# Weights of a 3x3 convolution behind two tiles' softmax, two small inputs by other queues, and a twelfth work tile

## The chip, the cores and the metric

The kernel runs on one core of one Trainium2 chip. The core has five engines that run side by side, each with its own queue that is worked through in order: TensorE (PE in the profile; its weight loads are PEld), VectorE (DVE), ScalarE (ACT), GpSimd (POOL) and SyncE (SP), which here only issues DMA transfers. GpSimd issues DMA transfers too. The engines wait for each other by semaphores. The metric is the time on the device in microseconds, the median of several runs; less is better. The profile shows one execution.

## The reference

The input x has the shape (2, 256, 64, 64). Two layers follow each other, each as x = x + layer(group norm of x), with 32 groups of 8 channels.

Layer 0 is self-attention with 8 heads of 32 channels over all 4096 positions of an image:

```python
qkv = einsum('bchw,oc->bohw', x, qkv_w) + qkv_b
w = softmax(einsum('bhci,bhcj->bhij', q, k) / sqrt(32), axis=-1)
out = einsum('bhij,bhcj->bhci', w, v)
```

Layer 1 has two branches on the same normalised input. The first is attention within sets of 64 positions, done twice: over positions 8 apart (queries and keys from 1x1 convolutions with a position term, then a 1x1 convolution, scale, shift and relu give `feats`), and then within 8 by 8 blocks, with two 1x1 convolutions and relu each for queries and keys, one for values, one for the output. The second branch mixes the heads of q, k and v by a 9 by 12 matrix and applies a grouped 3x3 convolution. The output is rate1 times the first branch plus rate2 times the second.

```python
f_all = einsum('bidn,oi->bodn', concatenate([qh, kh, vh], 1), fc_w)
out_conv = conv_general_dilated(f_conv, dep_w, (1, 1), ((1, 1), (1, 1)), feature_group_count=hd)
return rate1 * out_att + rate2 * out_conv
```

## The kernel before, in words

All of it is in `direct_layers`. Images are done one after the other (the batch index b is 0, then 1), each as eight tiles of 512 positions by 256 channels, two halves of 128 channels (KC = 2) on the partitions.

**Order of the work.** Pools give out buffers: `work` has 11 tiles of 4 KB per partition that everything short-lived shares (`w4`), `xpool` nine tiles of x, `const` what stays. A tile waits until the last reader of the buffer's previous tenant is done. The order of instructions on an engine is made by a scheduler from the program's order and its own estimates, except inside `manual_schedule`, which keeps the written order on the engines it names; `issue_after` sets an instruction behind another one. SP's and GpSimd's DMA issues stand in their queues like other instructions.

**Start.** SP loads the rows of w1 and w2 (L86), `place_rows` (L90) and the eight tiles of x (`load_x`, L70). GpSimd clears and loads small things: at_query, masks, `grid` (L169), at last `meet` (L209). `fold_scores` folds two 1x1 convolutions of layer 1 into one matrix: two transposes (L192), a small product, `meet` filled by ScalarE, a product of `meet` and `grid` (pt_key, L215), and the products pt_g (L204), copied to wt_g and kept in memory. VectorE meanwhile takes statistics of x (`group_stats`, L308, L312); their means over groups are a matmul (pm_l, L315), which follows the fold in TensorE's queue. Then VectorE normalises x (L350), and `project0` projects queries, keys and values (L400, L423).

**Attention of layer 0** (`attention0`): sixteen groups of scores, exponentials on ScalarE (L499), products with the values (L509), sums on VectorE (L546) and by adding DMA transfers of GpSimd (L556).

**Layer 1, first attention** (`layer1_first`). `group_attention` is a generator in parts: scores (sp, L1006), values (pvs, L988), softmax on VectorE and ScalarE (L1022 to L1029: nm, e, den); then transposes of the weights (at, L1034) and their copy into `bd` (L1043); then the products pc (L1052). In batch 0, `conv_weights` is called after it. It makes the 3x3's weights: three small loads, products with the mixing matrix, and for each half of the channels 9 taps of 12 scaled additions (L845, L847), then sums and differences of the taps (L851 to L858). The result goes to memory by 32 stores of SP (L860). `kept["made"]` is the last of these operations.

**Layer 1, second attention and convolution** (`layer1_second`). For each tile t, `branch` makes queries (phq, prq: L1262, L1271), another call makes keys (phk, prk), then come scores, softmax, at and pc as above. Between these stand the 16 steps of the convolution, four positions of four strips, where `spots` says: place 0 after the queries, 1 after the scores, 2 after pc. A step (`conv`) makes the next strip's input on GpSimd (`conv_transform`: L911 col, L915 v), then 32 matmuls (mm, L925), a copy by ScalarE and sums on VectorE (z, L930 to L934; into x, L946 to L952). All mm use one accumulator, so one waits for the z of the last. The first step loads all weights back (L875), transposes them on TensorE (pw, L884) and scales them (L887, L889). `to_image` (ScalarE, L1221) writes the padded image xp, whose first row VectorE clears in batch 0 (L1213). `conv_edges` (L959) corrects the borders of x by small additions. When a strip's four steps are done, its two output tiles are finished (L1321) and stored (L1324), which also frees x for batch 1: SP loads the next x (L70), and VectorE takes its statistics (L308).

Of the kernel before, what the change touches and what calls it, by code (L numbers as in the profile page):

```python
# [17 lines left out]
P = 128  # L18
# [4 lines left out]
KC = C // P  # L23
# [17 lines left out]
def direct_layers(ctx: ExitStack, tc: tile.TileContext, a: dict, out: bass.AP, bad: bass.AP):  # L41
# [7 lines left out]
    apool = ctx.enter_context(tc.tile_pool(name="apool", bufs=1))  # L49
    kpool = ctx.enter_context(tc.tile_pool(name="kpool", bufs=2))  # L50
    vpool = ctx.enter_context(tc.tile_pool(name="vpool", bufs=1))
    work = ctx.enter_context(tc.tile_pool(name="work", bufs=11))
    small = ctx.enter_context(tc.tile_pool(name="small", bufs=2))
    wpool = ctx.enter_context(tc.tile_pool(name="wpool", bufs=3))
    cpool = ctx.enter_context(tc.tile_pool(name="cpool", bufs=1))
# [24 lines left out]
    for name in ("w1", "w2"):  # L80
        by_out[name] = wpool.tile([P, KC, C], F32, tag="wp", name=f"{name}_by_out")

        for i in range(4):
            for half in range(2):
# [1 line left out]
                nc.sync.dma_start(  # L86
                    out=by_out[name][r : r + 32, i // 2, :], in_=a["wx"][int(name == "w2"), half, i, 0:P:4, :]
                )
    place_rows = const.tile([4, C], F32, name="place_rows")
    nc.sync.dma_start(out=place_rows, in_=a["posq"])  # L90
    x_first = load_x(0)

    ident = const.tile([P, P], F32, name="ident")
# [71 lines left out]
    nc.gpsimd.memset(at_query, 0.0)  # L165
    masks = const.tile([P, 2], F32, name="masks")
    nc.gpsimd.memset(masks, 0.0)
    grid = const.tile([2, 64], F32, name="grid")
    nc.gpsimd.dma_start(out=grid, in_=a["loc"][1:3, 0:64])  # L169
    for u in range(4):  # L170
        r = HD0 * u
        for half in range(2):
# [11 lines left out]
    def fold_scores():  # L184


        wts["g"] = wpool.tile([P, KC, C], F32, tag="wp", name="wt_g_0")

        place = const.tile([P, KC, 4], F32, name="place")
        pp = bank([P, KC, 4], "pt_place")  # L190
        for k in range(KC):
            nc.tensor.transpose(pp[:, k, :], place_rows[:, k * P : (k + 1) * P], ident[0:4, 0:4])  # L192
        nc.scalar.copy(place, pp)

        part = const.tile([P, KC, 3], F32, name="query_part")
        for k in range(KC):
            nc.scalar.activation(
                part[:, k, 0:1], place[:, k, 0:1], AF.Identity, bias=place[:, k, 3:4], scale=0.125
            )
        nc.scalar.copy(part[:, :, 1:3], place[:, :, 1:3])  # L200

        def product(dst, lhs, rhs):
            for j in range(KC):
                nc.tensor.matmul(dst, lhs(j), rhs(j), start=j == 0, stop=j == KC - 1)  # L204

        pm = bank([2, 3], "pt_meet")
        product(pm, lambda j: place[:, j, 1:3], lambda j: part[:, j, :])
        meet = const.tile([2, P], F32, name="meet")
        nc.gpsimd.memset(meet, 0.0)  # L209
        by_four = meet.rearrange("j (u r) -> j u r", u=4)  # L210
        nc.scalar.copy(by_four[:, :, 0:2], ident[0:2, 0:2].unsqueeze(1).to_broadcast([2, 4, 2]))
        for u in range(4):
            nc.scalar.copy(by_four[:, u, 2:AT], pm)
        pk = bank([P, 64], "pt_key")
        nc.tensor.matmul(pk, meet, grid, start=True, stop=True)  # L215
        nc.scalar.copy(at_key, pk)
        for k in range(KC):
            block = slice(k * P, (k + 1) * P)
            pg = bank([P, C + AT], f"pt_g_{k}")
            product(pg[:, 0:C], lambda j: by_out["w1"][:, j, block], lambda j: by_out["w2"][:, j, :])  # L220
            product(pg[:, C : C + 2], lambda j: by_out["w1"][:, j, block], lambda j: place[:, j, 1:3])
            product(pg[:, C + 2 : C + AT], lambda j: by_out["w2"][:, j, block], lambda j: part[:, j, :])
            nc.scalar.copy(wts["g"][:, k, :], pg[:, 0:C])
            nc.scalar.copy(w_at[:, k, 0:AT], pg[:, C : C + AT])
        nc.sync.dma_start(out=kept_w["g"], in_=wts["g"])
# [842 lines left out]
    def layer1_first(b, xts, put, check, st):  # L1068
# [129 lines left out]
                before = parts  # L1198

        load_set(b, ("fq1", "fk1", "fv"))  # L1200
        if b == 0:
            with tc.issue_after(done.ins):
                kept["bias"] = conv_weights()
        return feats, mean, rstd, shift

    def layer1_second(b, xts, feats, mean, rstd, shift, pacc):

        xp = apool.tile([P, KC, PADW, PADW], F32, tag="A", name=f"xp_{b}")
        for k in range(KC):
            if b == 0:  # L1210

                with tc.issue_after(kept["made"].ins):
                    nc.vector.memset(xp[:, k, 0, :], 0.0)  # L1213
            else:
                nc.gpsimd.memset(xp[:, k, 0, :], 0.0)
            nc.gpsimd.memset(xp[:, k, PADW - 1, :], 0.0)
            nc.gpsimd.memset(xp[:, k, 1 : PADW - 1, 0 : PADW : PADW - 1], 0.0)

        def to_image(t):
# [10 lines left out]
        wf = None  # L1230


        spots = {t: (0, 1, 2) for t in range(2, 7)} | {1: (1,)} if b == 0 else {
            t: (0, 1, 2) if t < 2 else (0, 1) for t in range(NT - 1)
        }
        images = {1: range(5), 2: (5, 6), 3: (7,)} if b == 0 else {0: (3, 4), 1: (5,), 2: (6,), 3: (7,)}

        def conv():
            nonlocal done, wf
            if wf is None:  # L1240
                wf = fetch_conv_weights(b)
            if done + 1 < len(turns):
                ahead[done + 1] = conv_transform(b, xp, *turns[done + 1])
            conv_step(b, xts, wf, ahead.pop(done), *turns[done], pacc)
            done += 1
# [6 lines left out]
        for t in range(NT):  # L1252
            nt = f"sr_{b}_{t}"
            f = [
                feats[k][:, 8 * t : 8 * t + 8].rearrange("p o d e -> p (o d e)") for k in range(KC)
            ]

            def branch(one, two, col1, col2, nm):
                hid = w4([P, KC, T], f"h{nm}_{nt}")
                ph = [bank([P, T], f"ph{nm}_{nt}_{m}") for m in range(KC)]  # L1260
                for k, m in ((0, 0), (0, 1), (1, 0), (1, 1)) if t == 0 else ((0, 0), (1, 0), (0, 1), (1, 1)):
                    nc.tensor.matmul(  # L1262
                        ph[m], wts[one][:, k, m * P : (m + 1) * P], f[k], start=k == 0, stop=k == KC - 1
                    )
                    if k == KC - 1:
                        bn_relu(hid[:, m, :], ph[m], col1, m)
                res = w4([P, KC, T], f"r{nm}_{nt}")
                pr = [bank([P, T], f"pr{nm}_{nt}_{m}") for m in range(KC)]
                for k in range(KC):
                    for m in range(KC):  # L1270
                        nc.tensor.matmul(  # L1271
                            pr[m], wts[two][:, k, m * P : (m + 1) * P], hid[:, k, :], start=k == 0, stop=k == KC - 1
                        )
                for m in range(KC):
                    bn_relu(res[:, m, :], pr[m], col2, m)
                return res

            with tc.manual_schedule(engines={mybir.EngineType.PE}):
                q = branch("fq1", "fq2", V_FQ1, V_FQ2, "q")
                if pending:  # L1280
                    next(pending)
                    next(pending, None)
                    pending = None
                for tt in images.get(t, ()):
                    to_image(tt)
                if b == 0 and t == 1:
                    ahead[0] = conv_transform(b, xp, *turns[0])
                if 0 in spots.get(t, ()):
                    conv()
                k = branch("fk1", "fk2", V_FK1, V_FK2, "k")  # L1290
                res = w4([P, KC, T], f"res_{nt}")

                def to_res(m, pc, res=res):

                    bn_relu(
                        res[:, m, :].rearrange("p (d o e) -> p o d e", d=8, o=8),
                        pc.rearrange("p (o d e) -> p o d e", o=8, d=8), V_SRW, m,
                    )

                parts = group_attention(  # L1300
                    nt, q, k, lambda c, w, f=f: f[c][:, w * P : (w + 1) * P], wts["fv"], to_res, apart=t + 1 < NT
                )
                next(parts)
                if 1 in spots.get(t, ()):
                    conv()
                if t == 0 and b == 0:
                    pending = parts
                else:
                    next(parts)
                    next(parts, None)  # L1310
                if 2 in spots.get(t, ()):
                    conv()
            for tt in ((), (0, 1))[t] if b == 0 and t < 2 else (t,):
                conv_edges(xts, tt)
            if b == B - 1 and t == 2:
                report()
            results[t] = res
            for n in sorted(n for n in results if done >= 4 * (n // 2 + 1)):
                res = results.pop(n)
                for m in range(KC):  # L1320
                    nc.vector.scalar_tensor_tensor(  # L1321
                        res[:, m, :], res[:, m, :], wts["rate1"], xts[n][:, m, :], ALU.mult, ALU.add
                    )
                nc.sync.dma_start(  # L1324
                    out=out[b, :, n * T : (n + 1) * T].rearrange("(k p) n -> p k n", p=P), in_=res
                )
# [584 lines left out]
```

## Time and profile before

| what | us |
|---|---|
| median of 3 runs | 3151.33 (3150.15 to 3154.11) |
| the profiled execution | 3150.88 |
| its span in the profile | 3149.1 |
| TensorE busy | 3039.4 |
| VectorE busy | 2472.8 |
| ScalarE busy | 2298.8 |
| GpSimd busy | 845.7 |

A row of the timeline gives the start in us from the beginning of the span, the time that the row covers, engine, line of the kernel, operation, output and inputs, shapes, and how many instructions are merged in it. Behind it in brackets is the idle time of the engine before it, with what ended that. The names in a row are those of the program's tiles, without their numbers. A wait for several things is put down to the one that came last by the profile. A row of the waits gives the sum, the number and the longest.

### The profile page before, as it was taken

To read this page: it belongs to the slowest core of one execution; us is meant where nothing else is said; L and a number is where in the kernel's file an instruction comes from. 1 tells how busy PE (TensorE), PEld (TensorE's weight loads), DVE (VectorE), ACT (ScalarE), POOL (GpSimd) and SP (SyncE) were. 2 spreads that over 40 slices of the span, in tenths; PEclk is the share of its full clock that TensorE was granted. 3 is DMA by queue.
4 is the path that set the end of the run, shared out by engine and by line. 5 is a ranking of instruction groups with operands and counts; after the bars stand their busy time and mean duration, and the time that the engine had idled before them with its cause. 6 is when DMAs were issued, how large, how long until landed. Compare 5 with 4: busy or idle time off the path is not lost. (4 is left out here: it accounts for less than half of the span.)

```text
span 3149.1 us, 62530 instructions
## 1 busy us (share of the span) xinstructions
PE 3039.4 (97%) x25049; PEld 1831.2 (58%) x25049; DVE 2472.8 (79%) x3204; ACT 2298.8 (73%) x2352; POOL 845.7 (27%) x947
## 2 busy tenths in 40 slices
PE   6999999999999999799999999999999999999998
PEld 3555555555555556577655555555555555467765
DVE  4489988999999998946544899889998999935543
ACT  2499999999999984432235999999999999834232
POOL 3022222222223231145300222222222222305530
PEclk9999999999999999999999999999999999999999
DMA  6979678796887761221049796787978976600000
GB/s 223 264 140 184 136 162 162 158 187 138 173 175 157 146 132 35 83 101 54 27 169 265 139 187 134 158 169 154 183 147 165 176 159 134 165 15 7 21 14 22
DMA packets 242756, 426.48 MB, mean 135 GB/s; under 512 B 99108, under 2 KB 109912, under 8 KB 240024
## 3 DMA queue, kind: packets, MB, share of 16 engines
q0 software_dynamic: 96400, 240.46, 39.8%
q1 hardware_dynamic: 146056, 181.94, 21.3%
q8 instruction: 198, 3.24, 0.4%
q14 instruction: 102, 0.84, 0.1%
HBM read 119.03 MB, written 68.39 MB: 60 GB/s over the span
## 5 line engine op out<-in xcount | busy, mean ns | idle before, releaser
L546 DVE TENSOR_TENSOR e<-e,es 128x1024 f32<-128x1024 f32 (+1 forms) x952 | 1035.1, 1142 | 85.8 <-ACT es L499 84.0
L509 PE MATMUL av<-es,v 128*32 128x256 f32 (+1 forms) x9644 | 748.1, 391 | 0.0
L546 DVE TENSOR_TENSOR e<-e,v 128x1024 f32<-128x1024 f32 (+1 forms) x640 | 675.8, 1109 | 53.8 <-ACT v L499 52.8
L499 ACT ACTIVATE es<-sa 128x1536 f32<-128x1536 f32 (+1 forms) x444 | 635.8, 1432 | 96.3 <-PE sa L493 55.8
L493 PE MATMUL sa<-q,k 128*128 128x512 f32 x1736 | 561.5, 430 | 11.6 <-issue 4.5
L509 PE MATMUL av<-v 128*32 128x256 f32 (+1 forms) x6228 | 506.5, 389 | 0.0
L509 PEld LDWEIGHTS av<-es,v 128*32 128x32 f32 x9644 | 316.5, 109 | 301.1 <-issue 163.1
L493 PEld LDWEIGHTS sa<-q,k 128*128 128x128 f32 x1736 | 280.2, 188 | 295.1 <-issue 142.0
L493 PE MATMUL sc<-q,k 128*128 128x512 f32 x1180 | 372.7, 397 | 8.8 <-ACT es L499 6.6
L493 PE MATMUL sb<-q,k 128*128 128x512 f32 x1180 | 370.6, 395 | 0.7 <-ACT v L499 0.7
L509 PEld LDWEIGHTS av<-v 128*32 128x32 f32 x6228 | 216.5, 109 | 178.8 <-issue 81.4
L499 ACT ACTIVATE es<-sc 128x1024 f32<-128x1024 f32 x296 | 307.0, 1037 | 6.1 <-DMA v<-es 6.1
L499 ACT ACTIVATE v<-sc 128x1024 f32<-128x1024 f32 x294 | 305.2, 1038 | 1.8 <-DMA acc<-v 0.9
L499 ACT ACTIVATE es<-sb 128x1024 f32<-128x1024 f32 x296 | 302.1, 1021 | 1.4 <-DMA acc<-es 1.4
L499 ACT ACTIVATE v<-sb 128x1024 f32<-128x1024 f32 x294 | 300.2, 1021 | 1.4 <-DMA acc<-v 1.4
L493 PEld LDWEIGHTS sc<-q,k 128*128 128x128 f32 x1180 | 210.1, 188 | 81.5 <-ACT es L499 18.1
L493 PEld LDWEIGHTS sb<-q,k 128*128 128x128 f32 x1180 | 220.8, 188 | 55.5 <-ACT v L499 1.5
L499 ACT ACTIVATE v<-sa 128x1536 f32<-128x1536 f32 (+1 forms) x146 | 209.2, 1433 | 36.7 <-PE sa L493 14.6
L925 PE MATMUL mm<-v,wf 128*128 128x256 f32 x1024 | 229.3, 382 | 3.9 <-DVE z L934 3.9
L556 POOL DMA_DIRECT2D es<-es x118 | 100.8, 855 | 473.7 <-ACT es L499 407.4
L925 PEld LDWEIGHTS mm<-v,wf 128*128 128x128 f32 x1024 | 194.5, 191 | 39.7 <-issue 13.3
L915 POOL TENSOR_TENSOR v<-col 128x512 f32<-128x512 f32 x128 | 161.3, 1288 | 204.5 <-PE mm L925 44.0
(262 smaller groups left out, 3181.4 us busy)
## 6 DMA issues: line engine op xcount, KB each, us to landing
acc<-es POOLq DMA_DIRECT2D x130, 512.0 KB, 6.4
acc<-v POOLq DMA_DIRECT2D x84, 512.0 KB, 6.2
es<-es POOLq DMA_DIRECT2D x138, 256.0 KB, 4.4
v<-es POOLq DMA_DIRECT2D x134, 256.0 KB, 5.1
k<-wk_halves SPq DMA_DIRECT2D x64, 512.0 KB
q<-wq_halves SPq DMA_DIRECT2D x256, 128.0 KB
v<-v POOLq DMA_DIRECT2D x90, 256.0 KB, 5.2
es<-v POOLq DMA_DIRECT2D x86, 256.0 KB, 4.0
```

Of the source, the lines that this page charges most:

```text
L493: nc.tensor.matmul(sc[:, i, :], held["k", g // 2][:, j * P : (j + 1) * P], held["q", g, u // 2][:, u % 2, :], start=True, stop=True,)
L499: nc.scalar.activation(dst, sc[:, i : i + m, :], AF.Exp, scale=SC0)
L509: nc.tensor.matmul(dst[HD0 * u : HD0 * u + HD0, n], lhs, rhs(u)[:, n], start=start, stop=stop)
L546: nc.vector.tensor_add(dst[:, s, :], dst[:, s, :], src)
L556: nc.gpsimd.dma_start(out=dst, in_=src, accum_op=ALU.add)
L915: (nc.gpsimd.tensor_add if plus else nc.gpsimd.tensor_sub)(dst, rows(one), rows(two))
L925: nc.tensor.matmul(mm[:, m, r, :], wf[:, k, 4 * r + q, m * P : (m + 1) * P], v[r // 2][:, r % 2, k, :], start=k == 0, stop=k == KC - 1,)
```

## The change

- `grid` and `meet` are made ahead of the loads of x: `grid` is loaded by SP instead of GpSimd, `meet` cleared by VectorE instead of GpSimd. `place_rows` is a work tile instead of a constant.
- `work` has 12 tiles instead of 11.
- `conv_weights` is called in `layer1_second`, after tile 1, with the same `issue_after` as before; the clearing of xp's first row and the first `conv_transform` follow it there.
- The softmax of tile 1 too is left open (`t < 2` instead of `t == 0`): its at and pc stand behind the queries of the next tile.
- The step of the convolution in tile 1 is gone and there is one in tile 7, so that each step stands one place later; `to_image` of tiles 5 to 7 is one tile later.

The order of instructions on the engines, as built, differs in these places. On TensorE: at, pvs and pc of tile 1 stand behind phq and prq of tile 2 and ahead of pw; and every mm one place later. On VectorE: the softmax of tile 0 and its bd stand further ahead within the operations of `conv_weights`, that of tile 1 near its end, and 13 of `conv_edges` between the clearing of xp and bd of tile 1. On GpSimd: w_at, ones and bd are cleared ahead of at_query's loads. On SP: kept_g and the loads of w3 and fq1 stand ahead of the first x of batch 1.

```diff
-    work = ctx.enter_context(tc.tile_pool(name="work", bufs=11))
+    work = ctx.enter_context(tc.tile_pool(name="work", bufs=12))
...
-    place_rows = const.tile([4, C], F32, name="place_rows")
+    place_rows = w4([4, C], "place_rows")
     nc.sync.dma_start(out=place_rows, in_=a["posq"])
+    grid = const.tile([2, 64], F32, name="grid")
+    nc.sync.dma_start(out=grid, in_=a["loc"][1:3, 0:64])
+    meet = const.tile([2, P], F32, name="meet")
+    nc.vector.memset(meet, 0.0)
     x_first = load_x(0)
...
-    grid = const.tile([2, 64], F32, name="grid")
-    nc.gpsimd.dma_start(out=grid, in_=a["loc"][1:3, 0:64])
...
-        meet = const.tile([2, P], F32, name="meet")
-        nc.gpsimd.memset(meet, 0.0)
...
         load_set(b, ("fq1", "fk1", "fv"))
-        if b == 0:
-            with tc.issue_after(done.ins):
-                kept["bias"] = conv_weights()
+        kept["seam"] = done.ins
         return feats, mean, rstd, shift
...
         for k in range(KC):
-            if b == 0:
-
-                with tc.issue_after(kept["made"].ins):
-                    nc.vector.memset(xp[:, k, 0, :], 0.0)
-            else:
+            if b:
                 nc.gpsimd.memset(xp[:, k, 0, :], 0.0)
...
-        spots = {t: (0, 1, 2) for t in range(2, 7)} | {1: (1,)} if b == 0 else {
+        spots = {t: (0, 1, 2) for t in range(2, 7)} | {7: (0,)} if b == 0 else {
             t: (0, 1, 2) if t < 2 else (0, 1) for t in range(NT - 1)
         }
-        images = {1: range(5), 2: (5, 6), 3: (7,)} if b == 0 else {0: (3, 4), 1: (5,), 2: (6,), 3: (7,)}
+        images = {1: range(5), 3: (5, 6), 4: (7,)} if b == 0 else {0: (3, 4), 1: (5,), 2: (6,), 3: (7,)}
...
-                if b == 0 and t == 1:
-                    ahead[0] = conv_transform(b, xp, *turns[0])
                 if 0 in spots.get(t, ()):
                     conv()
...
-                if t == 0 and b == 0:
+                if t < 2 and b == 0:
                     pending = parts
                 else:
                     next(parts)
                     next(parts, None)
                 if 2 in spots.get(t, ()):
                     conv()
+            if b == 0 and t == 1:
+                with tc.issue_after(kept["seam"]):
+                    kept["bias"] = conv_weights()
+                with tc.issue_after(kept["made"].ins):
+                    for k in range(KC):
+                        nc.vector.memset(xp[:, k, 0, :], 0.0)
+                ahead[0] = conv_transform(b, xp, *turns[0])
```

## The prediction

> **What bounds the kernel now.** I read the busy table of the page first, then the waits of TensorE, then the timeline around each long wait. The page:
>
> ```profile
> span 3149.1 us, 62530 instructions
> PE 3039.4 (97%) x25049; PEld 1831.2 (58%) x25049; DVE 2472.8 (79%) x3204; ACT 2298.8 (73%) x2352; POOL 845.7 (27%) x947
> ```
>
> TensorE lacks 3149.1 − 3039.4 = 109.7 us of being busy throughout. The change adds no work to it and takes none away, so what it can win lies in these gaps. The waits of TensorE say where they are (columns: us in total, times, longest):
>
> ```profile
> PE pt_key L215 <- DMA at_query<-in_loc_dram: 17.7, 1, 17.7
> PE pm_l L315 <- DVE mv_l L312: 9.0, 2, 6.8
> PE at_sr L1034 <- DVE e_sr L1029: 9.0, 1, 9.0
> PE pc_sr L1052 <- DVE bd L1043: 6.4, 3, 3.4
> PE mm L925 <- DVE z L934: 3.9, 1, 3.9
> PE pw L884 <- DMA wf<-wf_kept: 2.9, 1, 2.9
> ```
>
> They belong to three places: the start, the first tiles of batch 0's second attention (the seam), and one wait of the convolution near the end of batch 0. The timeline of the start:
>
> ```profile
> 27.86 0.58 DVE L312 BATCH_NORM_AGGREGATE mv_l<-stats_l 128x2 f32<-128x48 f32 x2
> 28.08 0.19 POOL L209 MEMSET meet<- 2x128 f32 x1
> ...
> 28.82 0.66 PE L215 MATMUL pt_key<-grid,meet 2*128 2x64 f32 x2 [17.69 <-DMA at_query<-in_loc_dram]
> ...
> 36.25 0.57 PE L315 MATMUL pm_l<-mv_l,group 128*128 128x2 f32 x2
> ```
>
> The statistics are ready at 28.44, but their matmul stands in TensorE's queue behind the fold, which waited for the memset of `meet`, last of GpSimd's small work. That row names at_query's DMA, yet reads only `grid` and `meet`. The first projection starts at 39.38. The timeline of the seam:
>
> ```profile
> 1310.10 7.21 DVE L847 SCALAR_TENSOR_TENSOR prep<-prep 128x256 f32<-128x256 f32 x18
> ...
> 1321.37 0.42 DVE L1022 TENSOR_REDUCE nm_sr<-sp_sr 128x4 f32<-128x256 f32 x1
> 1325.15 0.69 PE L1034 MATMUL at_sr<-ident,e_sr 128*128 128x128 f32 x2 [9.00 <-DVE e_sr L1029]
> 1331.21 0.19 DVE L1213 MEMSET xp<- 128x66 f32 x2
> 1332.14 5.39 DVE L959 TENSOR_SCALAR x<-x,edges 128x8 f32<-128x8 f32 x5
> 1333.80 4.92 POOL L915 TENSOR_TENSOR v<-col 128x512 f32<-128x512 f32 x4
> 1335.95 0.33 SPq L875 DMA_DIRECT2D wf<-wf_kept  x1
> 1348.19 8.87 PE L884 MATMUL pw<-ident,wf 128*128 128x128 f32 x64 [2.90 <-DMA wf<-wf_kept]
> ```
>
> The scores of tile 0 end at 1309.1, their softmax starts at 1321.37: VectorE's queue has the weights of the 3x3 ahead of it. A second chain runs from the last weight (1331.2) through their way to memory to the load of all of them (issued 1335.95) and the transposes (1348.19).
>
> **What the Trainium skill says.** "TensorE: Matmul & The Clock Gate", What's actually happening: the array falls to half clock after an idle window of about 3.4 us and needs about as long to return. The trace agrees: after the 9.0 us wait eight matmuls of L988 took 3.18 us, elsewhere 1.89; but here a 2.9 us wait was enough, since the first transposes come at 0.85 us for four, later ones at 0.44. "GPSIMD Engine Reference", Specifications: GpSimd shares its SBUF interfaces with VectorE and contends with 2-port modes and two SBUF inputs. It agrees: beside GpSimd's L915 five 8-column L959 took 5.39 us; four without it took 0.68 (at 1369.77).
>
> **The change part by part.** All times in this part are on the clock of before.
>
> Start. `meet` is cleared by VectorE as its first instruction (about 0.2 us, idle then: VectorE waits for x until 12.50). `grid` goes on SP's queue between `place_rows` and x: one issue, 0.37 to 0.45 us, and x and so the statistics are that much later. GpSimd loses one DMA issue (0.52) and one memset, for which nobody waits then. The key matmul can run at about 11.6 (after pt_meet, 10.88), the fold of some 7 us (29.40 to 36.2) ends by 19, and pm_l runs when the statistics are there: 28.5 + 0.45 = 29.0 instead of 36.25. Gain 7.2. All inputs of the first projection are there (VectorE reads the last x at 27.9, and GpSimd's waits for wk, wq and wv end by 23.1). Behind it TensorE has no gap until 127, so the gain carries. SP takes kept_g and w3 ahead of the first x of batch 1; nobody waits for these. Bounds: 0 if the folded weights' loads were late, though they are issued by 8.1 and nothing waits for them now except inside the hidden fold; 7.8 without the x delay. I take 7.2.
>
> Seam, TensorE. The order of after: phq, prq of tile 1 to 1316.0 as now; then at, pvs, pc of tile 0 without the 9.0 wait, 4.2 (1398.59 to 1402.82): 1320.2; phk to sp of tile 1, 9.8 (1381.82 to 1391.58): 1330.0; phq, prq of tile 2, which stood behind the transposes, 6.9: 1336.9; at and half of the values of tile 1: 1339.0.
>
> Seam, VectorE. From 1307.99 to the memset at 1331.21 it now needs 23.2. The softmax of tile 0 is inside already, but moved forward. New inside: a wait for the scores, 0.9; the two bd copies of tile 0, 0.85; the softmax of tile 1, 1.45; four more edge additions, 0.5. Sum 3.7: memset at 1334.9. Then 4.75 to the issue of wf (as 1331.2 to 1335.95; SP's 32 stores keep their order) and 12.24 for the load: 1351.9. Twelve work tiles and `place_rows` as one of them cost nothing here; no tile that TensorE needs there waits for its buffer.
>
> Between memset and bd of tile 1 the order of after has 13 edge additions (L959), while GpSimd starts its L911 and L915. Some three slip in before it; the others go one to each GpSimd operation, ten of them, of 1.24 and 2.14 us: bd done about 1350.4. Lower bound 0.14 each, and bd waits only for at (1337.3). So pc of tile 1 starts at 1350.4 and takes 3.35 cold: 1353.8, a little later than wf. Transposes 16 × 0.44 and 0.5 of warming: 1361.3; one mm of 6.9: 1368.2, and phk of tile 2 follows. At that point before has also done mm_0_1, another 6.9 us: 1381.82 − 6.9 = 1374.9. Gain 6.7; with unhindered edges wf decides, 1351.9 + 8.7 cold + 6.9, gain 7.4. What is late next is therefore these weights themselves: some 11 of the 15.3 us idle stay, under pc and pw.
>
> Convolution one place later. Each of 16 steps moves one spot, the last into tile 7. Now, four times, finished output tiles free x buffers for batch 1, and VectorE's statistics of them stall its queue until the DMA lands. Once that costs TensorE:
>
> ```profile
> 1538.43 1.34 SPq L70 DMA_DIRECT2D x<-in_x_dram  x2
> ...
> 1542.85 0.69 DVE L308 BATCH_NORM_STATS2 stats_l<-x 128x6 f32<-128x512 f32 x1 [4.33 <-DMA x<-in_x_dram]
> ...
> 1545.73 8.83 PE L925 MATMUL mm<-v,wf 128*128 128x256 f32 x32 [3.90 <-DVE z L934]
> ```
>
> 3.9 idle and 8.83 − 7.07 = 1.76 of half clock, 5.7 together; that place (tiles 4, 5) gets the spacing which tiles 0, 1 have now, free of a stall. But tiles 2, 3 get the spacing that stalled, with a statistics instruction inside z_2_0. There are no edge additions among the output there (2.4 us before): stall about 3.9 − 2.4 = 1.5 and no half clock. Gain 5.7 − 1.5 = 4.2, taken as 4.0; bounds 0 and 5.7.
>
> End of batch 0. The last mm stands before phk of tile 7, so the last x of batch 1 lands some 12.7 us after it, and its statistics are ahead of the values' copy and bd: 0.7 later; bounds 0 and 3. Batch 1 keeps its order.
>
> Sum: −7.2 − 6.7 − 4.0 + 0.7 = −17.2. The profiled execution took 3150.88 us (1.8 around its span); 3150.88 − 17.2 = 3133.7. The median of the runs, 3151.33, lies 0.45 above it: 3134.
>
> **Rivals.** (1) The start wins little: x or the folded weights arrive later, or the first stores fill the DMA engines (75% busy from 50 to 100 us) and TensorE stops there. For it: 16 tiles of 0.5 MB in 27.5 us are 305 GB/s. Against: TensorE has no wait there now. Gain 1 instead of 7: 3140. (2) The seam wins nothing: stores and load of the weights take 6 longer beside other traffic, or edges do: 3141. For it: wf decides pw anyway. Against: the DMA queues are empty then. (3) More: no stall at tiles 2, 3, nor at the end, and edges slip through: 3131 and, with a faster chain of stores, 3129. (4) Slower: attention on twelve work tiles. Its loads of queries take work tiles, so with one tile more they can start earlier, among the transfers that copy and add exponentials; these are then late, ScalarE waits for their buffers and TensorE for ScalarE. For it: DMA engines are 80% busy there, and ScalarE waits for "DMA v<-es" (6.1 us in all) now. Against: the order of SP's queue in attention is the same, and from 300 to 1000 us TensorE is busy 697.69 of 700. There are 32 groups; 0.54 us each eats the 17.2, and from (17.2 + 6.3) / 32 = 0.73 us each on it is slower by more than 0.2%; at 0.8, 3160. (5) No difference, by about 0.5 us each of the same: 3150. The edges under GpSimd can't do it: its third transform waits for pc of tile 1 after eleven operations, some 16 us, and then VectorE is free.
>
> **How the numbers follow.** Forecast 0.62 (3131 to 3138), (1) 0.11, (2) 0.13, (3) 0.08, (4) 0.03, (5) 0.03. No change can be told within 0.2%, 6.3 us, that is between 3145 and 3157.6. Faster 0.94, same 0.03, slower 0.03. The range 3128 to 3142 takes in (1) to (3) but for their tails.
>
> **What would show it.** pm_l near 29 and the first p_wk near 32; no wait of at_sr for e_sr at the seam; softmax of tile 0 about 3 us after its scores started, within the weights; L959 stretched to over 1 us each beside L911 and L915, TensorE idle about 11 us at pc_sr or pw, pw near 1346.6 on the new clock (1353.8 − 7.2); mm waiting for z once, for 1 to 2 us, near 1479 (1499.98, where mm_2_2 stands now, less 6.9 for one mm fewer before it, 6.7 and 7.2). Wrong it would be if pw started past 1352 there, or if a gap opened between 40 and 127.

## The result, and the profile after

The kernel after takes 3140.56 us, the median of 7 runs (3138.81 to 3143.24), against 3151.41 us before (7 runs). The ratio is 0.9966, with a 95% interval from 0.9954 to 0.9978: faster by 10.8 us, 7 to 14.5 by the interval. The forecast was 3134, 17.3 less, with a range of 3128 to 3142. The direction holds, and so does the range, but only because it took in rivals (1) and (2), put at 3140 and 3141: the band of the forecast itself, 3131 to 3138, was missed. More than a third of the gain is missing, and the question of the study is where it went.

The busy table of the page:

```profile
span 3141.1 us, 62513 instructions
PE 3037.7 (97%) x25049; PEld 1831.2 (58%) x25049; DVE 2484.0 (79%) x3205; ACT 2298.8 (73%) x2352; POOL 849.5 (27%) x945
```

Of TensorE's waits (us in total, times, longest) the ones that answer to those shown of before:

```profile
PE pm_l L315 <- DVE mv_l L312: 18.7, 3, 9.6
PE pc_sr L1052 <- DVE bd L1043: 11.6, 3, 6.7
...
PE mm L925 <- DVE z L934: 4.5, 2, 3.9
...
PE pw L884 <- DMA wf<-wf_kept: 2.8, 1, 2.8
```

The long waits of pt_key (17.7 before) and of at_sr for e_sr (9.0) are gone. Two have grown: pm_l, which now comes first in the queue, waits 9.6 us for the statistics themselves, and pc_sr waits longer for bd. The wait of mm for z is still there. The timeline of the start (start, time covered, engine, line, operation; idle before in brackets):

```profile
11.67 0.69 PE L215 MATMUL pt_key<-grid,meet 2*128 2x64 f32 x2 [0.40 <-ACT meet L213]
...
28.92 0.59 PE L315 MATMUL pm_l<-mv_l,group 128*128 128x2 f32 x2 [9.65 <-DVE mv_l L312]
...
32.07 13.30 PE L400 MATMUL p_wk<-xn,wqk 128*128 128x512 f32 x27 [1.14 <-DVE xn L350]
```

The fold now lies under the loads of x, and the first projection starts at 32.07 instead of 39.38. The timeline of the seam:

```profile
1299.47 0.43 DVE L1022 TENSOR_REDUCE nm_sr<-sp_sr 128x4 f32<-128x256 f32 x1 [0.42 <-PE sp_sr L1006]
...
1306.25 0.38 PE L1034 MATMUL at_sr<-ident,e_sr 128*128 128x128 f32 x2
...
1325.65 2.14 POOL L911 TENSOR_TENSOR col<-xp 128x1152 f32<-128x1152 f32 x1 [51.01 <-DVE x L959]
1325.87 9.29 DVE L959 TENSOR_SCALAR x<-x,edges 128x8 f32<-128x8 f32 x9
...
1327.88 4.90 POOL L915 TENSOR_TENSOR v<-col 128x512 f32<-128x512 f32 x4
1328.44 0.33 SPq L875 DMA_DIRECT2D wf<-wf_kept  x1
...
1332.86 2.14 POOL L911 TENSOR_TENSOR col<-xp 128x1152 f32<-128x1152 f32 x1
...
1335.07 0.85 DVE L1043 COPY bd<-at_sr 64x256 f32<-64x256 f32 x2
1336.07 3.38 PE L1052 MATMUL pc_sr<-bd,vs_sr 128*128 128x128 f32 x16 [6.73 <-DVE bd L1043]
1342.29 8.84 PE L884 MATMUL pw<-ident,wf 128*128 128x128 f32 x64 [2.85 <-DMA wf<-wf_kept]
```

The softmax of tile 0 starts as soon as its scores are there (VectorE waits 0.42 us for them), and at_sr has no wait. Nine 8-column edge additions take 9.29 us beside GpSimd's L911 and L915, bd stands behind them, and TensorE idles 6.73 us ahead of pc. The load of the weights (issued at 1328.44) lets the transposes start at 1342.29.

In what follows, "tiles 2, 3" and "tiles 4, 5" are the pairs of output tiles that a strip of the convolution finishes; by then the second attention has come to tile 5 or 6. The timeline of the convolution at tiles 2, 3 and of the end of batch 0:

```profile
1464.67 7.66 DVE L1322 SCALAR_TENSOR_TENSOR res_sr<-res_sr,rate,x 128x512 f32<-128x512 f32 x4
...
1472.84 1.38 SPq L70 DMA_DIRECT2D x<-in_x_dram  x2
...
1477.59 0.69 DVE L308 BATCH_NORM_STATS2 stats_l<-x 128x6 f32<-128x512 f32 x1 [4.67 <-DMA x<-in_x_dram]
...
1480.48 9.71 PE L925 MATMUL mm<-v,wf 128*128 128x256 f32 x32 [3.91 <-DVE z L934]
...
1587.36 0.69 DVE L308 BATCH_NORM_STATS2 stats_l<-x 128x6 f32<-128x512 f32 x1 [2.52 <-DMA x<-in_x_dram]
...
1589.56 2.02 PE L1052 MATMUL pc_sr<-bd,vs_sr 128*128 128x128 f32 x16 [3.35 <-DVE bd L1043]
```

A statistics instruction of batch 1 waits 4.67 us for its DMA on VectorE, in the middle of the z of the step before (z_2_0). TensorE then idles 3.91 us ahead of mm, and the mm takes 9.71 us instead of 7.07: 6.6 us are lost at one place.

To see where time is won along the execution, take the start of one matmul in the profile of before, less its start in another profile. From phk of tile 2 to that of tile 6, a kernel with the shifted convolution has done one mm less (6.91 us), which is taken off there. Us won against before:

| start of | after | after, a second profile | start only | start and twelve tiles | after, statistics held |
|---|---|---|---|---|---|
| first p_wk | 7.3 | 7.3 | 6.4 | 7.3 | 7.6 |
| phk of tile 0 | 9.7 | 7.3 | 8.4 | 7.2 | 8.6 |
| phk of tile 2 | 17.0 | 17.8 | 9.6 | 10.8 | 19.2 |
| phk of tile 7 | 15.8 | 16.7 | 9.8 | 13.5 | 24.9 |
| p_wk of batch 1 | 14.0 | 16.8 | 9.9 | 13.6 | 25.0 |
| last pc | 10.5 | 15.2 | 6.8 | 11.2 | 24.8 |

The columns behind the first are the experiments below. Two profiles of the same kernel after differ by 2.4 us at phk of tile 0 and by 4.7 at the end, so differences of 2 to 3 us between single profiles carry nothing. A profiled execution isn't the median either: that of after (3143.21) is among the slowest of its seven. Between p_wk of batch 1 and the last pc the kernel with only the start changed loses 3.1, the kernel after 3.5 and 1.6, that with held statistics 0.2. So the loss there is not shown to be the change's; more likely the profile of before was a good one in that stretch.

### The profile page after: what moved, and what is told of

Read it like the earlier page. It is cut to its first block, busy times and chain, and to the rows that moved or that the text cites. A ratio compares the mean times of both kernels' runs of the same rounds, so it can differ in the third digit from the quotient of the medians.

```text
span 3141.1 us, 62513 instructions
## 1 busy us (share of the span) xinstructions
PE 3037.7 (97%) x25049; PEld 1831.2 (58%) x25049; DVE 2484.0 (79%) x3205; ACT 2298.8 (73%) x2352; POOL 849.5 (27%) x945
## 5 line engine op out<-in xcount | busy, mean ns | idle before, releaser
L915 POOL TENSOR_TENSOR v<-col 128x512 f32<-128x512 f32 x128 | 165.7, 1319 | 196.1 <-DVE x L946 44.1
```

Source lines behind the costliest of these rows:

```text
L915: (nc.gpsimd.tensor_add if plus else nc.gpsimd.tensor_sub)(dst, rows(one), rows(two))
```

## The experiments

Each edit is against the kernel before or after, as its text says. Each kernel was timed together with the kernel before, whose median moves between 3146.9 and 3151.4 from set to set, so it is the ratios to it that can be compared across sets.

**The three parts alone.** First the start:

```diff
+    grid = const.tile([2, 64], F32, name="grid")
+    nc.sync.dma_start(out=grid, in_=a["loc"][1:3, 0:64])
+    meet = const.tile([2, P], F32, name="meet")
+    nc.vector.memset(meet, 0.0)
     x_first = load_x(0)
...
-    nc.gpsimd.dma_start(out=grid, in_=a["loc"][1:3, 0:64])
...
-        nc.gpsimd.memset(meet, 0.0)
```

> The kernel before with only the start of the change: grid on SP's queue, meet cleared by VectorE. Theory A (the three parts of the change act each in its own place and add up): 7.3 us less before the first projection, 3143 to 3144.5; pm_l starts near 28.9. Theory B (the start only lengthens later waits of the first attention, and the gain comes from the seam): 3149 to 3151, with new gaps of TensorE before 300 us.

Measured: 3139.21 us, ratio 0.9963 (0.9950 to 0.9977). In its profile 6.4 us are won at the first p_wk, with no new gap behind it, so theory B falls. The median is below A's range: the runs show more than the trace, 7 to 16 us by the interval. Five runs from 3137.7 to 3145.0, of which the profiled one is the slowest, don't settle the size. Then the tiles:

```diff
-    work = ctx.enter_context(tc.tile_pool(name="work", bufs=11))
+    work = ctx.enter_context(tc.tile_pool(name="work", bufs=12))
-    place_rows = const.tile([4, C], F32, name="place_rows")
+    place_rows = w4([4, C], "place_rows")
```

> The kernel before with only twelve work tiles and place_rows as one of them. Theory A (twelve tiles cost nothing; what the kernel after lost in batch 1 differs between executions): within 1.5 us of before, 3150 to 3153. Theory C (the loss of some 3 us in batch 1 comes from the tiles): 3154 or more, with longer waits of ScalarE for es and acc in the attention.

Measured: 3147.81 us, ratio 0.9992 (0.9984 to 1.0001): the tiles cost nothing, theory C falls, and they may win a little. Its profile shows where. GpSimd's timeline of before at tiles 4, 5, where TensorE stalled:

```profile
1528.29 5.74 POOL L915 TENSOR_TENSOR v<-col 128x512 f32<-128x512 f32 x4 [6.67 <-PE pc_sr L1052]
```

and with twelve tiles, GpSimd and then TensorE:

```profile
1522.75 2.49 POOL L915 TENSOR_TENSOR v<-col 128x512 f32<-128x512 f32 x2 [3.67 <-PE mm L925]
1526.98 2.93 POOL L915 TENSOR_TENSOR v<-col 128x512 f32<-128x512 f32 x2 [1.74 <-PE pc_sr L1052]
...
1542.38 7.14 PE L925 MATMUL mm<-v,wf 128*128 128x256 f32 x32 [1.78 <-DVE z L934]
```

With one more tile half of GpSimd's L915 no longer waits for a buffer that pc frees, and so lies less beside the residual additions (L1321, which finish the output tiles). From the first of these to the issue of the next x it is 1535.10 − 1528.71 = 6.4 us instead of 8.5; the stall is 1.78 instead of 3.90, and mm stays at full clock. Then the third part, the kernel after without the new start:

```diff
-    grid = const.tile([2, 64], F32, name="grid")
-    nc.sync.dma_start(out=grid, in_=a["loc"][1:3, 0:64])
-    meet = const.tile([2, P], F32, name="meet")
-    nc.vector.memset(meet, 0.0)
...
+    nc.gpsimd.dma_start(out=grid, in_=a["loc"][1:3, 0:64])
...
+        nc.gpsimd.memset(meet, 0.0)
```

> The kernel after with the start undone: grid by GpSimd's queue and meet cleared by GpSimd. Theory A: 7.7 us won up to the keys' branch of tile 2, 0.9 lost again in the convolution by a stall at tiles 2 and 3 and 1.9 at the end of batch 0, so about 5 us less than before: 3145.5 to 3147.5. Theory B (the seam gives nearly all): 3141 to 3143. Theory C (the tiles cost 3 us): 3149 or more.

Measured: 3147.85 us, ratio 0.9991 (0.9984 to 0.9997), 1 to 5 us won. Theory B falls; A's 5 us is the upper end of the interval. This kernel has the tiles, the move of the weights and the shift, and is no faster than the tiles alone (3147.81, in the same set). The other way round, the kernel before with the first two parts is a base for the third:

> The kernel before with the start of the change and the twelve work tiles, without the weights' new place and without the shifted convolution: it stands against after for that part alone. Theory A (this part wins 7 to 8 us at the seam and loses 3 by the stalls at tiles 2, 3 and at the end): 3143 to 3145, 4 more than after. Theory E (on top of twelve tiles it wins nothing, since these already shorten the wait for z that the shift would have removed): 3138.5 to 3141.5, the same as after.

Measured: 3146.11 us, ratio 0.9980 (0.9971 to 0.9989). That is slower than the start alone (0.9963, five runs of another set), which the tiles should not make it; the intervals just overlap, and why is open. The kernel after, run beside it once more:

> The kernel after once more, beside the others of this set. Every theory: 3139 to 3142. Its profile tells what differs between executions of one program: the theory that the 3.5 us lost in batch 1 and the 2.4 us after the last matmul are scatter expects at least one of them to be more than 1.5 us smaller here; the theory that the change costs them expects both again.

Measured: 3140.11 us, ratio 0.9967 (0.9955 to 0.9979). By this pair the weights' move and the shift win 0.0013 of 3151, about 4 us, as theory A says, with intervals that just overlap; by the pair above, without the new start, they win nothing. So what these two parts are worth by the runs lies somewhere between 0 and 4 us. The start is clearer: after against the kernel without it wins 0.0025, about 8 us, and these intervals are apart.

In the second profile of after the loss in batch 1 is 1.6 instead of 3.5, the last pc starts 4.7 us earlier, and pc at the end of batch 0 waits 1.44 instead of 3.35: one program differs by as much between executions. From the start of the last matmul to the end it is over 11 us in both, 8.7 before and 9.6 to 11.6 in the seven others up to the one with four loads; why before's was so short is open.

The same starts of matmuls give the time that TensorE takes for each stretch, in us. Kernels with the shifted convolution have 6.91 for one mm added in the first row and taken off in the second:

| stretch | before | start only | twelve only | start and twelve | after | after, second | after without the start | after, statistics held |
|---|---|---|---|---|---|---|---|---|
| phk of tile 0 to phk of tile 2 (the seam) | 83.3 | 82.1 | 79.9 | 79.7 | 76.0 | 72.8 | 74.7 | 72.7 |
| phk of tile 2 to phk of tile 7 (the convolution) | 207.4 | 207.2 | 204.4 | 204.6 | 208.6 | 208.5 | 208.5 | 201.7 |
| phk of tile 7 to p_wk of batch 1 (the end) | 21.7 | 21.7 | 21.7 | 21.7 | 23.5 | 21.6 | 25.3 | 21.6 |

The second row is the steadiest. The twelve tiles alone win 3 us in it, and the shifted convolution, which has them too, loses these and 1 us more. The first row says that the seam is quicker by 4 to 7 us than with the tiles alone, and the third that its price at the end is 0 to 3.6. Over all three the three kernels with move and shift take 306.5 us in the mean, those with twelve tiles alone 306.0: what the seam wins on them, the shift and the end give back.

**The statistics in the convolution.** On VectorE the statistics of batch 1's x are set behind the second z of the next strip, those of the last tile behind bd of tile 7 (`kept["last"]` is the last operation of a z, `kept["copied"]` the last copy into bd):

```diff
+                kept["hold"].update({2 * s - 1: kept["last"], 2 * s: kept["last"]})
...
+            hold = kept.get("hold", {}).get(t)
+            with tc.issue_after(hold.ins) if hold else nullcontext():
+                for k in range(KC):
+                    st.tile(k, t)
...
+            kept["hold"][NT - 1] = kept["copied"]
```

> The kernel after with the statistics of batch 1's x held back on VectorE until the second z of the next strip, those of the last tile until the bd copies of tile 7. Theory A (the statistics' wait for the DMA makes the stall at tiles 2 and 3, and the late bd at the end of batch 0): the mm wait of 3.9 us and its cold matmuls (2.6) go, and 1.9 at the end: 6.5 to 8.4 less than after, 3132 to 3134. Theory D (z is late there because the residual additions beside GpSimd are slow, whatever the statistics do): the wait stays at 1 us or more, 3138 or more.

Measured: 3131.31 us, ratio 0.9939 (0.9925 to 0.9952), 8.5 less than after by the ratios, a little more than theory A's range. Its timeline at the same place:

```profile
1470.44 1.39 SPq L70 DMA_DIRECT2D x<-in_x_dram  x2
...
1472.03 0.68 DVE L936 TENSOR_TENSOR z<-z,mm 128x512 f32<-128x512 f32 x1
...
1474.03 7.07 PE L927 MATMUL mm<-v,wf 128*128 128x256 f32 x32
...
1487.78 2.46 DVE L308 BATCH_NORM_STATS2 stats_l<-x 128x6 f32<-128x512 f32 x4
```

x is issued as late as ever against mm, and the residual additions are as slow (7.64 us for four); but the last operation of z starts 1.6 us after the issue, and mm has no wait and full clock. Theory D falls: the stall is the statistics' wait. In the table of stretches the convolution takes 201.7 us instead of 208.5, and the end, which the same edit covers, 21.6.

**The seam.** The edge additions of tiles 0 and 1 go behind the first z, out of bd's way:

```diff
-            for tt in ((), (0, 1))[t] if b == 0 and t < 2 else (t,):
+            for tt in (t,) if b or t > 1 else ():
                 conv_edges(xts, tt)
...
+                    if b == 0 and t == 2:
+                        with tc.issue_after(kept["last"].ins):
+                            for tt in range(2):
+                                conv_edges(xts, tt)
```

> The kernel after with the edge additions of tiles 0 and 1 put behind the first z on VectorE, so that none stands between the memset of xp and the bd copies of tile 1. Theory F (bd's delay is covered, since the load of the weights lands later): bd near 1329 instead of 1335, the wait before pc shrinks by about 6.5 us and the wait before pw grows by as much, pw starts within 1 us of 1342: 3139.5 to 3142. Theory G (the edges set the seam): 3 us or more less, 3137 or below.

Measured: 3143.18 us, ratio 0.9971 (0.9960 to 0.9982). Nothing is won; the median is 1.2 us above theory F's range:

```profile
1328.38 0.86 DVE L1043 COPY bd<-at_sr 64x256 f32<-64x256 f32 x2 [2.19 <-PE at_sr L1034]
...
1330.75 1.60 PE L1052 MATMUL pc_sr<-bd,vs_sr 128*128 128x128 f32 x12 [0.23 <-ACT vs_sr L993]
1342.63 9.55 PE L884 MATMUL pw<-ident,wf 128*128 128x128 f32 x64 [10.28 <-DMA wf<-wf_kept]
```

bd and pc come 6 to 7 us earlier, and the idle time moves whole to pw: theory G falls, the load decides. Its transposes are even colder, 9.55 us. Next the load in four parts:

```diff
-        nc.sync.dma_start(out=wf, in_=wf_kept)
+        for g in range(4 if b == 0 else 1):
+            some = slice(4 * g, 4 * g + 4) if b == 0 else slice(0, UW)
+            nc.sync.dma_start(out=wf[:, :, some, :], in_=wf_kept[:, :, some, :])
```

> The kernel after with the load of the 3x3's weights in four parts of four positions each, so that the transposes of the first parts need not wait for the last. Theory F (the load of 13.6 us sets the end of the seam): pw starts behind pc at about 1339.5 without a wait, the first mm about 1346.5 instead of 1351: 3.5 to 4.5 less, 3136 to 3137.5. Theory H (the parts share the DMA engines and all land together at the end): no gain, 3139 to 3142.

Measured: 3136.11 us, ratio 0.9952 (0.9938 to 0.9965), 4 to 5 less than after, with intervals that overlap. TensorE's timeline, and behind it the same transposes in the second profile of after:

```profile
1335.02 3.75 PE L1054 MATMUL pc_sr<-bd,vs_sr 128*128 128x128 f32 x16 [6.72 <-DVE bd L1045]
1338.56 7.99 PE L886 MATMUL pw<-ident,wf 128*128 128x128 f32 x64
1346.39 7.07 PE L927 MATMUL mm<-v,wf 128*128 128x256 f32 x32
```

```profile
1343.16 7.18 PE L884 MATMUL pw<-ident,wf 128*128 128x128 f32 x64 [1.23 <-DMA wf<-wf_kept]
1350.17 7.07 PE L925 MATMUL mm<-v,wf 128*128 128x256 f32 x32
```

The transposes follow pc without a wait, as theory F says; now bd and the edges do decide. How much that wins depends on the execution it is held against. From phk of tile 0 to the first mm the first profile of after takes 62.2 us, its second, where the load was waited for only 1.23 us and the clock was full, 59.0, the kernel with held statistics 58.9, and this one 58.6. So four loads take away a wait that costs 3.6 us in one execution and 0.3 in two others; the 4 to 5 us of the runs are more than that, and their size stays open.

**Versions that beat both.** Held statistics and four loads together:

> The kernel after with both edits that won alone: statistics held back, and the weights loaded in four parts. They act in different places (the convolution's tiles 2, 3 and the end of batch 0; the seam). Theory A (they add up): some 8.5 and 4 less than after, 3126.5 to 3129. Rival: one takes the other's gain, 3131 or more.

Measured: 3130.16 us, ratio 0.9937 (0.9923 to 0.9951), and in a second set, with the expectation below, 3130.88 us, ratio 0.9941 (0.9928 to 0.9955).

> The kernel with held statistics and four loads once more, beside the other: 3128.5 to 3131.5 by every theory.

By the runs they win no more than the statistics alone (0.9939), and theory A, that the gains add up, is not borne out: both medians lie between its range and the rival's. The profile shows both edits at work, with no wait of pw for the load and none of mm for z. But from phk of tile 0 to phk of tile 2 this kernel takes 65.5 us in both profiles, and the kernel with held statistics and one load had taken 65.8: in that execution there was next to nothing left for the four loads to win. To fill the gap ahead of pc, the keys' branch of tile 2 is moved there:

```diff
                     next(pending)
+                    if t == 2:
+                        k = branch("fk1", "fk2", V_FK1, V_FK2, "k")
                     next(pending, None)
```

> The same with the keys' branch of tile 2 (16 matmuls, 7.0 us) moved ahead of pc of tile 1, where TensorE waits 6.7 us for the bd copies. Theory F (the gap at pc is idle time that other work can fill, and the transposes then wait at most for the last quarter): the wait before pc falls below 1 us, pc and the transposes run at full clock, and mm of the next step waits 1 to 2 us for z, since only values and scores are left between them: 4 to 6 less than without the move, 3121.5 to 3124. Rival (the transposes then wait for the load instead, or ScalarE's hk copies come too late): 1 less or nothing, 3126 or more.

Measured: 3130.62 us, ratio 0.9941 (0.9927 to 0.9954): nothing is won, as the rival says. The gap has moved into the branch:

```profile
1336.57 5.19 PE L1273 MATMUL prk_sr<-hk_sr,wt_fk 128*128 128x512 f32 x8 [3.33 <-DVE bd L1047]
1341.59 1.95 PE L1056 MATMUL pc_sr<-bd,vs_sr 128*128 128x128 f32 x16
```

prk needs a PSUM bank that at of tile 1 holds until bd is copied, and bd still stands behind the edges. So the edges go behind bd as well:

```diff
                     if t == 2:
+                        with tc.issue_after(kept["copied"].ins):
+                            for tt in range(2):
+                                conv_edges(xts, tt)
                         k = branch("fk1", "fk2", V_FK1, V_FK2, "k")
```

> The kernel with held statistics, four loads and the keys' branch of tile 2 ahead of pc, and now also with the edge additions of tiles 0 and 1 behind the bd copies of tile 1. Theory I (in the run without this the bd copies, late behind the edge additions, held the PSUM bank that the second half of the keys' branch needs, so the gap only moved): no wait of 1 us or more between at of tile 1 and the transposes, these end about 1346 with the keys' branch already done, so 7 less at the end of the first mm, of which the later waits of mm for z and of at for e_sr, with cold matmuls, take back about 5: 3126.5 to 3129. Rival J (the transposes wait for the load or for VectorE's copies of them, which now stand behind edge additions beside GpSimd): 3130 or more.

Measured: 3124.37 us, ratio 0.9926 (0.9912 to 0.9939), 19 to 28 us less than before and by the ratios 12.6 less than after, the best of all, and 2 us better than theory I. TensorE's timeline:

```profile
1333.49 3.60 PE L1273 MATMUL prk_sr<-hk_sr,wt_fk 128*128 128x512 f32 x8
1336.92 1.95 PE L1056 MATMUL pc_sr<-bd,vs_sr 128*128 128x128 f32 x16
1338.71 7.26 PE L888 MATMUL pw<-ident,wf 128*128 128x128 f32 x64
1345.81 7.07 PE L929 MATMUL mm<-v,wf 128*128 128x256 f32 x32
...
1366.24 0.44 PE L1038 MATMUL at_sr<-ident,e_sr 128*128 128x128 f32 x2 [2.55 <-DVE e_sr L1033]
```

From at of tile 1 to the first mm TensorE has no gap. Behind it, waits of 0.86 us of mm for z and of 2.55 us for the softmax of tile 2 are left. The edge edit, worth nothing alone, is worth about 5 us here (0.9926 against 0.9941 without it; its five runs, up to 3126.6, all lie below the five of held statistics and four loads in the same set, from 3127.3): its cover, the load, is gone.

## Why the prediction was right in direction and too large

**Step 1, the start: right.** pm_l was put at 29.0 and the first p_wk near 32; they are at 28.92 and 32.07, in the second profile within 0.1 of that. The gain of 7.3 is the predicted 7.2, and undoing the start costs about 8 us in the runs. Rival (1) falls: no gap opens between 40 and 127. (Its 305 GB/s were twice too high: the load of x is nine transfers of 512 KB, the last of them for batch 1, so that 8 × 0.524 MB in 27.5 us are about 150 GB/s.)

**Step 2, the seam: size about right, one rate wrong.** TensorE gained 7.3 us from phk of tile 0 to phk of tile 2 in one profile and 10.5 in the other, against 6.7; but the kernel with only start and tiles shows 3.6 there, so the figure is good to some 3 us. Of the working, the memset of xp and at of tile 1 came where they were put, within 0.1 us in the second profile (1327.71 and 1329.65, put at 1334.9 − 7.2 and 1336.9 − 7.2), and the weights' load landing last was right, as the first two runs on the seam show. pw was put at 1346.6 on the new clock and started at 1342.29. The rate of the edge additions was wrong: ten of the thirteen were put at one per GpSimd operation. Four ran before GpSimd's first operation or in its first 0.3 us (1325.39 to 1325.95). Of the nine behind them six each ended within 0.03 us of the GpSimd operation beside which they ran, 1.3 to 2.2 us long, as put; but three passed in 0.22 us each where GpSimd changes between L911 and L915. So they took six operations and not ten (why L959, which reads one tensor, is held up at all no view shows), and bd came at 1335.07 and not at 1343. This hid behind the load, as the bound with unhindered edges had allowed. Rival (2), a seam that wins nothing, falls by the profiles.

**Step 3, the convolution: this step failed.** It claimed a stall of 3.9 − 2.4 = 1.5 us at tiles 2, 3 without half clock, since there are no edge additions among the output there, and a gain of 4.0. Measured are 3.91 us of wait and 2.64 of half clock, and from phk of tile 2 to phk of tile 7 a loss of 1.2 and 1.1 us in the two profiles: 5.2 us off. The place was right to 1.5 us (near 1479, at 1480.48). The subtraction was wrong. The rows of VectorE in before (those of after stand above, at 1464.67):

```profile
1529.93 1.75 DVE L1321 SCALAR_TENSOR_TENSOR res_sr<-res_sr,rate,x 128x512 f32<-128x512 f32 x1
1531.61 2.46 DVE L959 TENSOR_SCALAR x<-x,edges 128x8 f32<-128x8 f32 x2
1533.97 3.95 DVE L1321 SCALAR_TENSOR_TENSOR res_sr<-res_sr,rate,x 128x512 f32<-128x512 f32 x3
```

Before, the stretch from the first residual addition to the issue of x was 1538.43 − 1529.93 = 8.5 us with two edge additions of 2.46; after, 1472.84 − 1464.67 = 8.2 without them, because the four residual additions alone took 7.66 us, 1.9 each, against 0.74 for one at the end of batch 0. Both stretches run beside GpSimd's five operations (four L915 of 5.7 to 6.2 us together, then L911) and end within 1.3 us of them, whatever VectorE holds between. This agrees with "GPSIMD Engine Reference" of the Trainium skill, Specifications: contention with VectorE instructions of two SBUF inputs, which L1322 is. That GpSimd's operations set the length is read from the traces, and the tiles bear it out: in the two kernels with twelve tiles but no shift two of the four L915 lie earlier, and the stretch is 6.4 us long. No run moved all of them away. That the waiting statistics are the stall is shown: with them held the loss is gone, and the runs give 8.5 us back, of which the stall's wait and clock are 6.6 and most of the rest lies at the end of batch 0.

What the forecast also missed is that the gain it gave to the shift was largely there without it: twelve tiles alone cut the stall at tiles 4, 5 to 1.78 us and win 3 us in this stretch. They were said to cost nothing, and that holds, but not to win anything. On top of them the shift loses 4 us, and all four L915 lie beside the residual additions again (6.20 us from 1463.02 on).

**Step 4, the end of batch 0: too small on the average.** Predicted +0.7 with bounds 0 and 3; 1.8 in one profile, none in the other, and 3.5 in the kernel without the new start. In the first profile of after it is the wait of pc for bd behind the last statistics, 3.35 us instead of 1.49; with the statistics held the end takes 21.6 us, as before.

**The sum.** Predicted −17.2. At p_wk of batch 1, up to which the change acts, the two profiles show −14.0 and −16.8, which is nearer than the runs' −10.8, but they start with 2.4 us and none that were won ahead of the seam, where nothing was changed. Rivals (4) and (5), a cost of each attention group, have nothing for them: twelve tiles alone are not slower. With the failed step put right, the sum is 17.2 − 5.2 = 12, and with some 1.7 us for the end instead of 0.7, the mean of three profiles, 11: inside the interval of 7 to 14.5. That it comes so near is in part luck, since each term is good to 1 to 3 us. The profiles' further loss, in batch 1 and behind the last matmul, is against one execution of before that was quick there.

## What to carry to other kernels

An instruction that waits for a DMA in an in-order queue stalls what stands behind it, and the wait counts from when the transfer is issued: ask what sets that issue, not how many instructions stand ahead. Where two engines hold each other up, as VectorE's additions and GpSimd's operations do here, a stretch can last as long as the other engine's list, and taking small work out of it then shortens nothing: look at what runs beside it. Before giving a gain to one part of a change, see whether another part has it already, as the twelve tiles had here. An edit that is worth nothing because another wait covers it can become worth several us once that cover is removed, so keep it and try it again.

## What the runs showed of the hardware that was not expected

- What a wait of TensorE costs in clock is not told by its length. The traces record the granted clock; behind the first one of each trace, every period of half clock lasted 3.41 us or two to five times that. Waits of mm for z of 3.66 to 4.11 us were followed by 8.83 to 10.12 us for the 32 matmuls, against 7.07. Ahead of the transposes, 2.90 us in the kernel before brought half clock, though 9.8 us at full clock stood ahead of it, as the prediction had read; 2.59 and 2.51 in the kernels with twelve tiles and no shift cost nothing (7.21 us for the 64); and after a pc at half clock 1.23 us went with 7.18 but 0.90, in the kernel without the new start, with 9.10. The rows of before for three stretches (from:to, length, then how long each engine was busy); the granted clock is the third figure from the end:

```profile
1345.30:1348.71 3.41, 0.52 (x5) 0.52 (x6) 2.49 (x5) 0.42 (x1) 3.25 (x3) 1.00 0.38 163
1348.71:1352.13 3.42, 3.42 (x19) 3.42 (x18) 1.38 (x2) 1.19 (x2) 2.05 (x2) 0.50 0.02 5
1352.13:1355.54 3.41, 3.41 (x33) 3.41 (x32) 2.70 (x4) 1.98 (x4) 0.00 (x0) 1.00 0.00 0
```

This fits the window of about 3.4 us of "TensorE: Matmul & The Clock Gate" of the Trainium skill, What's actually happening, which runs on by itself, so that a wait would count by where it falls. If the windows lie as these steps do, one need not be idle throughout: the 3.41 us ahead of the drop still held 0.52 us of matmuls. It also means that part of the scatter between profiles, 1.7 us at pw alone, is the clock's.

- Beside GpSimd the copies from PSUM were not slowed: the eight scaled copies of the transposes took 0.69 us each in every profile of the seam, also while L915 ran beside them in the run with four loads, and bd its usual 0.85 beside L915, while six of the nine 8-column additions in SBUF just ahead of it took 1.3 to 2.2 us instead of 0.22, each ending with GpSimd's operation beside it.
- One load of 4 MB, waited for as a whole, kept TensorE for 13.9 us in one profile of after (1328.44 to 1342.29) and 12.3 in the other (1330.87 to 1343.16); in four parts, issued within 2.64 us, the first part was there 11.2 us after the first issue at the latest (1327.40 to 1338.56), and the others came in time for their transposes.
